# A two-bank PSUM tile for the exponentials of two places in a selective-scan kernel

## The chip, the cores and the metric

The kernel runs on one core of a Trainium2 chip. The metric is device time in microseconds (us), the median of the runs shown. Five engines are spoken of: PE (TensorE, matmuls; PEld is its weight load), DVE (VectorE), ACT (ScalarE), POOL (GpSimd) and SP (SyncE, which issues the DMAs). SBUF is the on-chip memory; PSUM is the accumulator memory, used here as eight banks of 512 fp32 columns on 128 partitions. All data are fp32.

## What is computed

Two layers on an image batch of shape (4, 128, 128, 128). The change lies in the first, a selective-scan ("Mamba") block over the 16,384 tokens of each image, with 256 inner channels and 16 states for each channel. Cut to what matters:

```
u     = silu(causal_conv4(split(x_mlp @ in_proj)))          # 256 channels
dt, B, C = split(u @ x_proj)                                 # 8, 16, 16
delta = softplus(dt @ dt_proj + bias);  A = -exp(A_log)      # A: 256 x 16
h[t,d,s] = h[t-1,d,s] * exp(delta[t,d] * A[d,s]) + delta[t,d] * B[t,s] * u[t,d]
y[t,d]   = sum_s h[t,d,s] * C[t,s] + u[t,d] * D[d]
out   = (y * silu(z)) @ out_proj;   x1 = silu(groupnorm(out)) + x
```

The second layer (group norm, a 1x1 convolution, softmax weights, and a filter in the frequency domain done with matmuls) follows on x1; the change doesn't touch it.

## The kernel before

**Tiling.** Tokens are cut into 128 chunks of T = 512 (32 for each of 4 images). The recurrence has 256 x 16 = 4096 rows for each chunk, as 32 tiles of 128 rows by 512 tokens; a tile has 32 channels by 4 states. They are ordered as 2 halves j of the channels, 4 rotations r, and 4 places p. A place is a group of four states; `place(r, p)` says which group of 32 channels it meets. (j, r) is a *unit* of four tiles, eight units to a chunk, and each unit is two *pairs*: places 0 and 1, then places 2 and 3. So there are 1024 pairs of places 2 and 3 in all.

**Work on one tile.** `exps` (L384): ACT computes exp(delta * A) into a tile da. The tiles of places 1, 2 and 3 are in PSUM, in the pool `psd`, one buffer and one bank each (tags da1, da2, da3); that of place 0 is in SBUF, two buffers. A new tile of the same tag waits until every reader of the old one is done. `dbu` (L352): POOL multiplies delta * u by B for places 1 to 3 into hb; for place 0 PE transposes the product into the PSUM tile b0 (`dbu_turn`, L374). `scans` (L395): DVE runs the recurrence over 512 tokens with one scan instruction per tile (L411), starting from the state that the chunk before left. Then h * C: for places where `by_vector` holds, the scan has written its states in place over da, and DVE multiplies them by C into hb (L413), and ACT copies the last column, the state for the next chunk, into the tile st (L414). For the other places the states lie in an SBUF tile h, POOL multiplies (L418, both places in one instruction of 1024 columns if both are POOL's), and ACT copies the last column later (L506). `sums` (L421): PE adds the four tiles of a unit into y (L432).

`by_vector` (L346) gives places 2 and 3 to DVE, places 0 and 1 to POOL, with two exceptions for balance: in odd chunks without normalisation place 1 of one unit is DVE's, and in the 48 chunks where the group norm of the image before is woven in (`norming`, L337), place 2 of one unit is POOL's.

**Order.** The schedule is written out by hand. A loop over *slots* n, one for each pair, issues the phases "turn", "sums", "pe", "exps", "late", "act", "pool", "dbu", "early", "gate", "scans", "dve", "end" in this order (L502 to L506), and each engine works through its instructions in the order of issue. The exponentials of a pair are issued one slot before its scans, place 0's three slots before. In a slot of places 2 and 3 DVE gets: scan 2, scan 3, multiply 2, multiply 3. On ACT, the two copies of a pair's last columns are issued in its slot, and the exponentials of places 2 and 3 of the next unit follow in the next slot. Between them stand ACT's other steps of the chunk that is being prepared: silu (L238, L241), softplus (L274), the scaling of transposed products (L303), copies out of PSUM. Each switch between exp, silu and softplus is an ACT_TABLE_LOAD.

**Waits.** The framework puts in the semaphore waits: an instruction waits for the last writer of what it reads, and for readers of what it overwrites, on its own engine too. In the listing of the built program, multiply 2 waits for scan 2, multiply 3 for scan 3, each copy (L414) for the multiply that reads the same PSUM tile, and each exponential of places 2 and 3 for the copy that released its tile.

Of the kernel before, what the change touches and what calls it, by code (L numbers as in the profile page):

```python
# [26 lines left out]
F32 = mybir.dt.float32  # L27
AF = mybir.ActivationFunctionType
ALU = mybir.AluOpType
# [4 lines left out]
P = 128  # L34
T = 512
# [119 lines left out]
def block0(tc, s):  # L155
    nc, B, NCH, NH, NS, NG, ND, R, NX, KC, HALO, C, L, NF, DI = (
        s.nc, s.B, s.NCH, s.NH, s.NS, s.NG, s.ND, s.R, s.NX, s.KC, s.HALO, s.C, s.L, s.NF, s.DI,
    )
    NT = T // P
    with ExitStack() as ctx:  # L160
        def pool(name, bufs, **kw):
            return ctx.enter_context(tc.tile_pool(name=name, bufs=bufs, **kw))

        p1 = pool("p1", 1)
        p2 = pool("p2", 2)
# [6 lines left out]
        psd = pool("psd", 1, space=PSUM)  # L172
# [168 lines left out]
        def place(r, p):  # L341


            return (p - r) % ND

        def by_vector(k, j, r, p):  # L346

            if norming(k):
                return p > 1 and (j, r, p) != (1, 2, 2)
            return p > 1 or (k % 2 == 1 and (j, r, p) == (1, 2, 1))  # L350
# [16 lines left out]
        def pair(n):  # L367

            k, r = divmod(n, NP)
            u, p = divmod(r, ND // 2)  # L370
            j, r = divmod(u, NG)
            return k, j, r, 2 * p
# [11 lines left out]
        def exps(n, qs):  # L384

            k, j, r, p = pair(n)
            d = st[k]
            for q in qs:
                m = place(r, p + q)
                c = (j * NG + p + q) * ND + m  # L390
                da = (psd if p + q else p2).tile([P, T], F32, tag=f"da{p + q}", name=f"da{p + q}_{k}_{j}_{r}")
                nc.scalar.activation(da, d["delta", j][:, m, :], AF.Exp, scale=s.amat[:, c : c + 1])  # L392
                d["da", j, r, p + q] = da

        def scans(n):  # L395


            k, j, r, p = pair(n)
            d = st[k]
            hb = d["hb", j, r]  # L400
            das = [d.pop(("da", j, r, p + q)) for q in range(2)]
            dve = [q for q in range(2) if by_vector(k, j, r, p + q)]
            pool = [q for q in range(2) if q not in dve]
            last = d["last", j, r, p] = tiny.tile([P, 2], F32, tag=f"st{j}_{r}_{p}", name=f"st_{k}_{j}_{r}_{p}")
            if pool:
                h = p2.tile([P, 2, T], F32, tag="h", name=f"h_{k}_{j}_{r}_{p}", bufs=3)
            for q in range(2):
                b = hb[:, p + q, :] if p + q else d.pop("b0")
                init = 0.0 if k % NCH == 0 else st[k - 1]["last", j, r, p][:, q : q + 1]
                o = das[q] if q in dve else h[:, q, :]  # L410
                nc.vector.tensor_tensor_scan(o, das[q], b, init, ALU.mult, ALU.add)  # L411
            for q in dve:
                nc.vector.tensor_tensor(hb[:, p + q, :], das[q], d["C"][:, p + q, :], ALU.mult)  # L413
                nc.scalar.copy(last[:, q : q + 1], das[q][:, T - 1 : T])  # L414
            if pool:
                q = slice(pool[0], pool[-1] + 1)
                ps = slice(p + pool[0], p + pool[-1] + 1)
                nc.gpsimd.tensor_tensor(hb[:, ps, :], h[:, q, :], d["C"][:, ps, :], ALU.mult)  # L418
                todo[n + 1, "late"].append(partial(nc.scalar.copy, last[:, q], h[:, q, T - 1]))
# [71 lines left out]
        for n in range(n_chunks * NP):  # L491
            if n % 2 == 0:
                todo[n - 3, "early"].append(partial(exps, n, (0,)))
            todo[n - 1, "exps"].append(partial(exps, n, (1,) if n % 2 == 0 else (0, 1)))
            todo[n - 1, "turn"].append(partial(dbu_turn, n))
            todo[n, "scans"].append(partial(scans, n))
            if n % 2 == 0:
                todo[n - 2, "dbu"].append(partial(dbu, n // 2))
            else:
                todo[n + 2, "sums"].append(partial(sums, n // 2))  # L500
# [483 lines left out]
```

## Time and profile before

| | |
|---|---|
| Median of 3 runs | 7226.67 us (7223.53 to 7229.71) |
| Profiled execution, span from first to last instruction | 7219.4 us (its time apart from the span isn't given) |
| DVE busy | 6925.4 us, 96% |
| POOL busy | 6890.8 us, 95% |
| ACT busy | 6133.6 us, 85% |
| PE busy | 5935.8 us, 82% |
| Exponentials, L392 (ACT) | 4096 of 698 ns |
| Scans, L411 (DVE) | 4096 of about 1260 ns |
| Multiplies by C on DVE, L413 | 2040 of 672 ns |
| Copies of last columns, L414 (ACT) | 2040 of 159 ns |

A group row of the profile has the source line, engine and operation, the tiles written and read with their shapes, the count, then the busy time (us) and the mean duration of one (ns), then the engine's idle time just before them and what ended it. A timeline row has the start in us, the time from the first start to the last end, the line and operation, and the count of equal instructions that were merged into the row; in brackets stands the wait before it. Neighbouring instructions of one engine overlap a little: the profile's end of one lies after the start of the next where the next doesn't need its result.

### The profile page before, as it was taken

What the parts mean: (1) busy time and instruction counts of PE and PEld (TensorE: products, weight loads), DVE (VectorE), ACT (ScalarE), POOL (GpSimd) and SP (SyncE); (2) the same over time, 40 slices, a digit from 0 to 9 for tenths busy, and PEclk for the clock granted to TensorE, in tenths of its full rate; (3) what the DMA queues carried; (4) which work ended last, traced back from release to release, by engine and by line L of the source; (5) the groups of instructions that cost most, each with busy time, mean ns of one, the idle gap of its engine ahead of it and who ended that gap; (6) DMA issues with size and microseconds to landing.
All of it is one profiled execution on the core that took longest, in us unless ns stands there. A gap on an engine that the chain in (4) does not pass through costs nothing. (4 is left out here: it accounts for less than half of the span.)

```text
span 7219.4 us, 89408 instructions
## 1 busy us (share of the span) xinstructions
PE 5935.8 (82%) x25908; PEld 2629.2 (36%) x25908; DVE 6925.4 (96%) x8040; ACT 6133.6 (85%) x13583; POOL 6890.8 (95%) x3188
## 2 busy tenths in 40 slices
PE   7888888888878788888788788887787888868999
PEld 2333333322222233332222233332232323348999
DVE  7999999999999999999999999999999999978677
ACT  7888888888888888888888888888888888877876
POOL 7999999999999999999999999999999999977787
PEclk8888888888888898998888899998888898989999
DMA  6766676677777776777777777777787777768666
GB/s 151 160 159 160 151 165 159 151 165 172 180 192 178 182 172 161 175 169 170 190 179 192 174 160 176 171 160 187 179 192 181 169 173 169 161 167 240 183 169 164
DMA packets 864127, 1246.27 MB, mean 173 GB/s; under 512 B 78856, under 2 KB 318608, under 8 KB 863632
## 3 DMA queue, kind: packets, MB, share of 16 engines
q1 hardware_dynamic: 863488, 1240.28, 71.8%
q8 instruction: 204, 3.34, 0.2%
q14 instruction: 291, 2.38, 0.1%
q10 hardware_dynamic: 144, 0.26, 0.0%
HBM read 996.97 MB, written 243.27 MB: 172 GB/s over the span
## 5 line engine op out<-in xcount | busy, mean ns | idle before, releaser
L362 POOL TENSOR_TENSOR hb<-rdu,rB 128x1536 f32<-128x1536 f32 (+2 forms) x1536 | 3608.0, 2366 | 35.1 <-DMA rdu<-dd 32.1
L392 ACT ACTIVATE da<-rdelta,amat 128x512 f32<-128x512 f32 x4096 | 2786.1, 698 | 139.3 <-DVE h L411 134.5
L418 POOL TENSOR_TENSOR hb<-h,rC 128x1024 f32<-128x1024 f32 (+1 forms) x1072 | 2436.8, 2275 | 68.4 <-DVE h L411 53.9
L411 DVE TENSOR_TENSOR_SCAN da<-da,st,hb 128x512 f32<-128x512 f32 x1976 | 2417.4, 1265 | 22.1 <-ACT da L392 15.6
L432 PE MATMUL y<-hb,sel 128*32 128x512 f32 x8192 | 1337.9, 730 | 4.7 <-POOL hb L418 4.1
L382 PE MATMUL b<-ident,bt 128*128 128x128 f32 x4096 | 753.9, 307 | 673.5 <-DVE h L411 539.1
L413 DVE TENSOR_TENSOR hb<-da,rC 128x512 f32<-128x512 f32 x2040 | 1294.3, 672 | 3.0
L411 DVE TENSOR_TENSOR_SCAN h<-da,st,b 128x512 f32<-128x512 f32 x992 | 1256.2, 1266 | 1.5 <-PE b L382 1.5
L411 DVE TENSOR_TENSOR_SCAN h<-da,st,hb 128x512 f32<-128x512 f32 x1000 | 1249.9, 1254 | 1.4 <-ACT da L392 1.0
L233 PE MATMUL pp_cv<-xm,wck 128*128 128x512 f32 x2048 | 1061.0, 665 | 1.4 <-ACT xm L216 0.8
L303 ACT ACTIVATE bt<-pt_dut,xdt 128x256 f32<-128x256 f32 x2048 | 836.3, 470 | 186.0 <-PE pt_dut L292 185.8
L382 PEld LDWEIGHTS b<-ident,bt 128*128 128x128 f32 x4096 | 525.5, 154 | 1242.1 <-DVE h L411 902.5
L414 ACT COPY st<-da 128x1 f32<-128x1 f32 x2040 | 271.3, 159 | 495.0 <-DVE hb L413 494.7
L233 PEld LDWEIGHTS pp_cv<-xm,wck 128*128 128x128 f32 x2048 | 417.3, 215 | 706.5 <-issue 460.8
L767 POOL TENSOR_TENSOR wb<-wb,term 128x1040 f32<-128x1040 f32 x192 | 461.1, 2402 | 89.8 <-ACT term L761 78.6
L292 PE MATMUL pt_dut<-ident,du 128*128 128x128 f32 x1024 | 233.7, 339 | 299.9 <-ACT xdt L285 174.0
L428 PE MATMUL y<-u,diag 128*128 128x512 f32 x512 | 300.9, 671 | 149.7 <-DVE zs L442 147.6
L292 PEld LDWEIGHTS pt_dut<-ident,du 128*128 128x128 f32 x1024 | 132.5, 163 | 618.6 <-POOL du L311 492.3
L392 ACT ACT_TABLE_LOAD x262 | 336.1, 1283 | 11.8 <-DMA rdelta<-dd 7.1
L311 POOL TENSOR_TENSOR du<-delta,u 128x512 f32<-128x512 f32 x256 | 319.6, 1271 | 26.7 <-ACT delta L274 26.7
L432 PEld LDWEIGHTS y<-hb,sel 128*32 128x32 f32 x8192 | 173.3, 116 | 371.4 <-issue 278.0
L266 PE MATMUL pp_dt<-xd,wdt 8*128 8x512 f32 x512 | 281.9, 639 | 31.9 <-ACT pp_o L456 23.4
(145 smaller groups left out, 8082.0 us busy)
## 6 DMA issues: line engine op xcount, KB each, us to landing
rdelta<-dd SPq DMA_DIRECT2D x1024, 256.0 KB, 4.7
rdu<-dd SPq DMA_DIRECT2D x1024, 256.0 KB, 7.8
rC<-bc SPq DMA_DIRECT2D x512, 256.0 KB, 7.5
rB<-bc SPq DMA_DIRECT2D x512, 192.0 KB, 4.7
dd<-delta SPq DMA_DIRECT2D x256, 256.0 KB, 7.4
dd<-du SPq DMA_DIRECT2D x256, 256.0 KB, 5.9
ft<-in_filt_w SPq DMA_DIRECT2D x104, 520.0 KB, 6.9
ob<-o SPq DMA_DIRECT2D x128, 256.0 KB, 2.0
```

The costliest lines, as they stand in the source:

```text
L233: nc.tensor.matmul(ps["cv", j], w, d["xm"][:, t : t + T], start=t == 0, stop=t == KC - 1)
L292: nc.tensor.transpose(ps["dut"][:, 2 * t + j, :], d["du"][:, j, at : at + P], s.ident)
L303: nc.scalar.activation(d["bt"][:, 2 * h + t, :, q, :], src, AF.Copy, scale=d["xdt"][:, 2 * h + t, R + q : R + q + 1])
L311: nc.gpsimd.tensor_tensor(du, d["delta"][:, j, :], d["u"][:, j, :], ALU.mult)
L362: nc.gpsimd.tensor_tensor(hb[:, p : p + n, :], d["du", j][:, m : m + n, :], d["B"][:, p - 1 : p - 1 + n, :], ALU.mult)
L382: nc.tensor.transpose(b[:, t * P : (t + 1) * P], src, s.ident)
L392: nc.scalar.activation(da, d["delta", j][:, m, :], AF.Exp, scale=s.amat[:, c : c + 1])
L411: nc.vector.tensor_tensor_scan(o, das[q], b, init, ALU.mult, ALU.add)
L413: nc.vector.tensor_tensor(hb[:, p + q, :], das[q], d["C"][:, p + q, :], ALU.mult)
L418: nc.gpsimd.tensor_tensor(hb[:, ps, :], h[:, q, :], d["C"][:, ps, :], ALU.mult)
L432: nc.tensor.matmul(y[m * DG : (m + 1) * DG, :], s.sel, d["hb", j, r][:, p, :], start=False, stop=r == NG - 1)
L767: nc.gpsimd.tensor_tensor(wb, wb, u[n].terms[f], ALU.add)
```

## The change

The exponentials of places 2 and 3 get one PSUM tile of 128 x 2 x 512 (tag da23, two banks, one buffer) in place of two tiles of one bank each; the number of banks in use stays eight. Place q of the pair is the half `[:, q, :]`. Where both places are DVE's, one multiply of 1024 columns follows the two scans, and one ACT copy takes both last columns. Where only one place is DVE's, the code for it is as it was, on its half of the tile. Places 0 and 1 keep their tiles and their code.

```diff
             for q in qs:
                 m = place(r, p + q)
                 c = (j * NG + p + q) * ND + m
-                da = (psd if p + q else p2).tile([P, T], F32, tag=f"da{p + q}", name=f"da{p + q}_{k}_{j}_{r}")
+                if p == 0:
+                    da = (psd if q else p2).tile([P, T], F32, tag=f"da{q}", name=f"da{q}_{k}_{j}_{r}")
+                else:
+                    if q == 0:
+                        d["pair"] = psd.tile([P, 2, T], F32, tag="da23", name=f"da23_{k}_{j}_{r}")
+                    da = d["pair"][:, q, :]
                 nc.scalar.activation(da, d["delta", j][:, m, :], AF.Exp, scale=s.amat[:, c : c + 1])
                 d["da", j, r, p + q] = da
...
                 o = das[q] if q in dve else h[:, q, :]
                 nc.vector.tensor_tensor_scan(o, das[q], b, init, ALU.mult, ALU.add)
-            for q in dve:
-                nc.vector.tensor_tensor(hb[:, p + q, :], das[q], d["C"][:, p + q, :], ALU.mult)
-                nc.scalar.copy(last[:, q : q + 1], das[q][:, T - 1 : T])
+            if len(dve) == 2:
+                both = d.pop("pair")
+                nc.vector.tensor_tensor(hb[:, p : p + 2, :], both, d["C"][:, p : p + 2, :], ALU.mult)
+                nc.scalar.copy(last, both[:, :, T - 1])
+            else:
+                for q in dve:
+                    nc.vector.tensor_tensor(hb[:, p + q, :], das[q], d["C"][:, p + q, :], ALU.mult)
+                    nc.scalar.copy(last[:, q : q + 1], das[q][:, T - 1 : T])
             if pool:
```

## Prediction

> **What bounds the kernel now.** I read the windows view first, to see which engine is full in which stage; then VectorE's waits inside that stage; then the timeline of VectorE and of ScalarE at single pairs; last, groups by shape for the rate per column. The chain of waits covers only the last 12% of the span (the second layer) and says nothing of the scan stage, so it isn't used.
>
> The scan stage runs from 49 to 6400 us. Its row gives the length, then busy time (and count) of PE, PE's weight loads, DVE, ACT and POOL:
>
> ```profile
> 49.00:6400.00 6351.00, 5158.17 (x19617) 1898.99 (x19616) 6314.61 (x6610) 5492.87 (x12263) 6266.72 (x2862) 0.88 0.73 170
> ```
>
> DVE is idle for 6351.0 - 6314.6 = 36.4 us in 6351, POOL for 84.3. ACT has 858 us free. DVE's own waits in that window name few others (total us, times, longest):
>
> ```profile
> DVE da L411 <- ACT da L392: 17.5, 17, 2.0
> ...
> DVE h L411 <- POOL hb L362: 4.0, 2, 3.7
> DVE da L411 <- POOL hb L362: 2.0, 2, 1.1
> ```
>
> So DVE sets the end of this stage, with POOL close behind. What lengthens DVE's chain comes through whole; what shortens it can bring 84 - 36 = 48 us before POOL is as full as DVE is now. One unit of DVE work, two pairs of places:
>
> ```profile
> 3011.82 1.27 DVE L411 TENSOR_TENSOR_SCAN h<-da,st,b 128x512 f32<-128x512 f32 x1
> 3013.00 1.26 DVE L411 TENSOR_TENSOR_SCAN h<-da,st,hb 128x512 f32<-128x512 f32 x1
> 3014.18 2.44 DVE L411 TENSOR_TENSOR_SCAN da<-da,st,hb 128x512 f32<-128x512 f32 x2
> 3016.53 1.27 DVE L413 TENSOR_TENSOR hb<-da,rC 128x512 f32<-128x512 f32 x2
> 3017.71 1.27 DVE L411 TENSOR_TENSOR_SCAN h<-da,st,b 128x512 f32<-128x512 f32 x1
> ```
>
> Read starts, not durations. Two scans take 16.53 - 14.18 = 2.35 us, 1.175 each, though one lasts 1.265: the next instruction starts some 0.09 before the last one's end, as it doesn't need its result. Two multiplies take 17.71 - 16.53 = 1.18. The same view at a place where the multiply needs the scan just ahead of it (place 1 on VectorE, in odd chunks):
>
> ```profile
> 3000.47 1.25 DVE L411 TENSOR_TENSOR_SCAN da<-da,st,hb 128x512 f32<-128x512 f32 x1
> 3001.76 0.69 DVE L413 TENSOR_TENSOR hb<-da,rC 128x512 f32<-128x512 f32 x1
> 3002.37 2.46 DVE L411 TENSOR_TENSOR_SCAN da<-da,st,hb 128x512 f32<-128x512 f32 x2
> ```
>
> Here the start to start is 1.29, not 1.175: the overlap is gone. In all 88 such places of the trace the gap after the scan is +33 to +35 ns, against a median of -87 elsewhere. **A hand-off to the very next DVE instruction costs 122 ns.** The kernel before avoids it at places 2 and 3 by the order scan, scan, multiply, multiply.
>
> **What the Trainium skill says.** "VectorE: DVE Perf Modes", the section on the TRN2 errata, has a fixed cost per instruction beside one cycle per column, and gives (N+151)/0.96 ns for an fp32 tensor_tensor: 691 ns at 512. The trace has 672 (2040 of L413); the part of it that is paid per instruction is what one multiply less saves. The same page, "The DRAIN you can't avoid", says that a semaphore after each op costs nothing extra. The trace disagrees, by the 122 ns above, and I take the trace. "PSUM — Partial Sum Buffer", section on bank collisions, wants any two engines kept apart on one bank, reads included. The trace agrees: the state copies, which only read, wait for the multiply that only reads (494.7 us of L414's idle time).
>
> **The change part by part.** In the listing of the built programs, with what each instruction waits for, 976 of the 1024 pairs have both places on VectorE and change in full; in the other 48 (batch chunks with normalisation) place 2 stays on POOL.
>
> 1. *One multiply of 1024 columns for two.* Rate from the two shapes of L820:
>
> ```profile
> L820 DVE TENSOR_TENSOR pr<-sq,wb 128x390 f32<-128x390 f32 x256 | 132.5, 559 | 8.8
> L820 DVE TENSOR_TENSOR pr<-sq,wb 128x260 f32<-128x260 f32 x128 | 48.8, 423 | 2.2
> ```
>
> (559 - 423)/130 = 1.046 ns per column, so 512 more columns add 536 ns to a multiply's pitch of 590: 1126 against 1184 for two. Gain 58 ns; the bounds are 0 (crossing a bank costs as much as an instruction) and 90 (all that a multiply has over its columns is saved, with overlap). I take 58.
>
> 2. *The second scan now waits for the first.* This isn't in the diff. The pair is one tile, and in the listing scan 3 waits for DVE's own count of scan 2, in all 976 pairs (before: none); the two touch different halves. Cost 122 ns, by the row above; bounds 0 (if a scan's result needs no wait, as the skill's sentence has it) and 150. I take 122.
>
> 3. *The multiply now follows the scan that it needs.* Before, one multiply stood between. In the listing all 976 wait for the instruction just ahead. Again 122 ns, same bounds.
>
> Sum on DVE per pair: 122 + 122 - 58 = +186 ns, times 976 = 181.5 us. The 48 other pairs keep their single multiply, already a hand-off, and get only the scan's wait: 48 x 0.122 = 5.9. Together **+187 us**, all on the path. One small wait of DVE for the second old multiply goes; it is done a unit earlier and costs nothing.
>
> 4. *State copy, 976 fewer on ACT.* L414 takes 159 ns, but two together take only 0.20 us, so about 40 to 60 ns each of ACT's time: some 50 us, on an engine with 858 free. Worth nothing by itself.
>
> 5. *Both exponentials wait for the one copy, and scan 2 for both exponentials.* The exponentials of the next unit may start only when the tile is released. Queued behind the waiting exponentials on ACT is everything in its order: silu, softplus, bt scaling, the next place 1. Before, in a quiet unit:
>
> ```profile
> 3011.93 0.16 ACT L414 COPY st<-da 128x1 f32<-128x1 f32 x1 [0.44 <-DVE hb L413]
> 3011.99 1.31 ACT L392 ACTIVATE da<-rdelta,amat 128x512 f32<-128x512 f32 x2
> ```
>
> The multiply ends at 3011.90; after it DVE runs two scans and reaches scan 2 at 3014.18, 2.28 us later. Now: copy 0.03 + 0.16, a hand-off of 0.03 on ACT (DVE's gap; ACT's copy to exponential shows the same), exponential 0.70, hand-off 0.03 (the second waits for the first, also in the listing), 0.70, and 0.03 to DVE: 1.68 us. It fits, with 0.6 to spare, where scan 2 had 1.5 before. The cover is a punctual ACT. It is gone after the table loads:
>
> ```profile
> 3017.88 1.31 ACT L392 ACTIVATE da<-rdelta,amat 128x512 f32<-128x512 f32 x2
> 3019.21 1.28 ACT L241 ACT_TABLE_LOAD   x1
> ...
> 3022.73 1.28 ACT L392 ACT_TABLE_LOAD   x1
> 3024.03 0.69 ACT L392 ACTIVATE da<-rdelta,amat 128x512 f32<-128x512 f32 x1
> ...
> 3025.53 1.30 ACT L392 ACTIVATE da<-rdelta,amat 128x512 f32<-128x512 f32 x2
> ```
>
> ```profile
> 3026.57 1.26 DVE L411 TENSOR_TENSOR_SCAN da<-da,st,hb 128x512 f32<-128x512 f32 x1
> ```
>
> The last two exponentials start at 3025.53, 1.24 after their multiply's end. The first is done at 3026.22, in time for 3026.57; the second, serial, at about 3026.96. Scan 2 then starts near 3026.99, 0.42 late. Both chains shift by nearly the same before that (ACT some 0.2 by its later start, DVE 0.19 by points 1 to 3), so the lateness stays. I made this sum for all 1023 successive pairs of the trace: (start of the exponentials, at least 0.23 after the multiply's end) + 1.46 - (start of scan 2). It is positive in 244: 123 at (half 1, rotation 0), after softplus, 0.28 each; 77 at (0, 2), after silu, 0.43 each; 27 at (1, 2), 0.61 each; 17 elsewhere. Sum **96 us**, bounded by 0 (DVE's slower pace gives ACT time) and 170 (0.3 more for each of the 244).
>
> 6. *What else moves.* POOL, PE and DMA issue the same instructions in the same order per unit and all get slack; DVE's waits for POOL (6 us) go. No queue is passed by a moved DMA.
>
> Sum: 187 + 96 - 6 = +277 us. The profiled execution spans 7219.4, 7.3 below the median of the three runs shown, 7226.67, so the difference is added to the median: **7504 us**.
>
> **Rivals.** *Hand-offs alone* (+187 - 6): ACT catches up because DVE is slower. For it, ACT has 14% free; against, the late units are late by bursts of table loads, not by the average. 7408. *Punctual ACT runs out*: the 0.6 us of slack is also eaten in quiet units by ACT work that sits ahead of the copy, say 0.1 us at the other 780: +277 + 78, 7582. Against it: the median start of the exponentials is 90 ns after the multiply. *Faster*: the hand-offs overlap after all, since the two scans touch different banks, so only the 58 ns of each multiply counts: -57 us, of which 48 fit before POOL is as full as DVE was; 7175. It decides if two hand-offs cost less than 58 ns, 29 each; the 88 places at +35 ns speak against it. That the two products are not merged is excluded by the listing (976 multiplies of 1024).
>
> **Chances.** Forecast 0.66, with its own range 7440 to 7560; hand-offs alone 0.16; ACT running out 0.12; faster 0.04; within 0.2% of no change (hand-offs at a quarter of their price) 0.02. A measurement here can tell about 0.2%, 14 us, from no change. The range reaches to 7400, takes in the hand-offs alone, and to 7580: it leaves out faster, same and most of the third case. Slower 0.94, same 0.02, faster 0.04.
>
> **What would show it.** In the changed trace: the multiply of 1024 columns at 1.21 us, starting some 35 ns after scan 3's end; scan 3 as far behind scan 2; scan 2 to the next scan 0 at 3.72 us, not 3.53; DVE's waits for ACT near 100 us, up from 19, mostly at two of the eight units of a chunk; POOL's busy share in the stage down to about 94%. If the scans still start 1.175 apart, points 2 and 3 are wrong and the sum with them; if DVE's waits for ACT stay at 20 us, point 5 is.

## The result, and the profile after

The changed kernel takes 7580.37 us (median, 7578.58 to 7584.86) against 7225.45 for the kernel before in the same session: a ratio of 1.0492, 95% interval 1.0479 to 1.0505, or 355 us more. The forecast was 277 us more, 7504; the measured time lies 0.4 us above the end of the range, 7580, and 76 us above the forecast itself. The direction and the mechanisms came as forecast, and one price, that of a hand-off on DVE, was too low.

The windows view of the scan stage, which now runs from 48 to 6760 us (length, then busy time of PE, weight loads, DVE, ACT and POOL):

```profile
48.00:6760.00 6712.00, 5315.78 (x19616) 1940.45 (x19618) 6507.55 (x5635) 5559.38 (x11288) 6275.63 (x2862) 0.85 0.68 161
```

The stage is 361 us longer. POOL's busy time is what it was within 9 us, so it isn't the bound: its share fell to 93.5%. DVE is busy for 193 us more, with 975 instructions fewer, and idle for 6712.0 - 6507.6 = 204 us where it was idle for 36. Its waits in the stage, by what ended them (only gaps over 0.15 us are listed):

```profile
DVE da L416 <- ACT da L397: 40.4, 40, 2.3
...
DVE da L416 <- issue: 33.9, 79, 1.2
DVE da L416 <- POOL hb L362: 20.5, 18, 1.6
```

All three are scans of places 2 and 3. What is put down to "issue" belongs mostly to ACT's bursts too: without table loads, below, that row falls from 33.9 to 8.4. The rest of DVE's 204 us is in gaps too short for this view. The timeline of one quiet unit of DVE (no burst on ACT, nothing else between the scans) shows them; the row after it, two scans of the unit that follows, is used further below:

```profile
3008.77 1.27 DVE L416 TENSOR_TENSOR_SCAN h<-da,st,b 128x512 f32<-128x512 f32 x1
3009.95 1.26 DVE L416 TENSOR_TENSOR_SCAN h<-da,st,hb 128x512 f32<-128x512 f32 x1
3011.13 2.59 DVE L416 TENSOR_TENSOR_SCAN da<-da,st,hb 128x512 f32<-128x512 f32 x2
3013.76 1.22 DVE L419 TENSOR_TENSOR hb<-da,rC 128x1024 f32<-128x1024 f32 x1
3014.90 1.27 DVE L416 TENSOR_TENSOR_SCAN h<-da,st,b 128x512 f32<-128x512 f32 x1
...
3017.26 2.66 DVE L416 TENSOR_TENSOR_SCAN da<-da,st,hb 128x512 f32<-128x512 f32 x2
```

The first two scans start 1.18 apart, as before. Scan 2 to the multiply, two hand-offs, takes 13.76 - 11.13 = 2.63 us where it took 2.35. The multiply of 1024 columns takes 14.90 - 13.76 = 1.14 where two took 1.18. The unit takes 6.13 us where it took 5.89. On ACT the chain from the released tile to the next unit's scan 2 is there as costed:

```profile
3015.01 0.16 ACT L420 COPY st<-da 128x2 f32<-128x2 f32 x1 [1.05 <-DVE hb L419]
3015.21 1.42 ACT L397 ACTIVATE da<-rdelta,amat 128x512 f32<-128x512 f32 x2
```

The multiply ends at 3014.98; the copy starts 0.03 later, the two exponentials lie end to end (1.42, not 1.31) and end at 3016.63, in time for scan 2 at 3017.26 in this unit.

**Where the time went.** Summing starts to starts over the 1023 units that have a successor, in both traces, splits the stage without a rest (where there are two multiplies, "its multiply" is the first):

| from start to start | before, us | after, us | difference | forecast |
|---|---|---|---|---|
| scan 0 to scan 1 | 1218.2 | 1216.6 | -1.6 | 0 |
| scan 1 to scan 2 (ACT late) | 1414.2 | 1520.3 | +106.1 | +96 |
| scan 2 to scan 3 | 1206.3 | 1358.4 | +152.1 | +125 |
| scan 3 to its multiply | 1205.8 | 1354.2 | +148.4 | +119 |
| multiply to the next scan 0 | 1301.3 | 1257.2 | -44.1 | -57 (and -6, POOL) |
| sum | 6345.9 | 6706.7 | +360.8 | +277 |

### The profile page after: what moved, and what is told of

It reads as the page before. It is cut to its first block, busy times and chain, and to the rows that moved or that the text cites. A ratio compares the mean times of both kernels' runs of the same rounds, so it can differ in the third digit from the quotient of the medians.

```text
span 7576.8 us, 86828 instructions
## 1 busy us (share of the span) xinstructions
PE 6091.0 (80%) x25908; PEld 2668.1 (35%) x25908; DVE 7117.8 (94%) x7064; ACT 6200.2 (82%) x12607; POOL 6899.9 (91%) x3188
## 5 line engine op out<-in xcount | busy, mean ns | idle before, releaser
L397 ACT ACTIVATE da<-rdelta,amat 128x512 f32<-128x512 f32 x4096 | 2867.7, 700 | 173.2 <-DVE h L416 102.7
L416 DVE TENSOR_TENSOR_SCAN da<-da,st,hb 128x512 f32<-128x512 f32 x1976 | 2537.6, 1284 | 153.8 <-ACT da L397 35.2
L382 PE MATMUL b<-ident,bt 128*128 128x128 f32 x4096 | 782.7, 315 | 880.7 <-DVE h L416 730.6
L442 PE MATMUL y<-hb,sel 128*32 128x512 f32 x8192 | 1395.6, 759 | 3.6 <-DVE hb L419 2.7
L419 DVE TENSOR_TENSOR hb<-da,rC 128x1024 f32<-128x1024 f32 x976 | 1195.0, 1224 | 33.2
L233 PE MATMUL pp_cv<-xm,wck 128*128 128x512 f32 x2048 | 1091.5, 681 | 1.4 <-ACT xm L216 0.8
L420 ACT COPY st<-da 128x2 f32<-128x2 f32 x976 | 152.2, 156 | 706.9 <-DVE hb L419 706.7
L397 ACT ACT_TABLE_LOAD x262 | 336.1, 1283 | 12.0 <-DMA rdelta<-dd 7.4
```

The lines of the kernel that those rows point to most:

```text
L233: nc.tensor.matmul(ps["cv", j], w, d["xm"][:, t : t + T], start=t == 0, stop=t == KC - 1)
L382: nc.tensor.transpose(b[:, t * P : (t + 1) * P], src, s.ident)
L419: nc.vector.tensor_tensor(hb[:, p : p + 2, :], both, d["C"][:, p : p + 2, :], ALU.mult)
L442: nc.tensor.matmul(y[m * DG : (m + 1) * DG, :], s.sel, d["hb", j, r][:, p, :], start=False, stop=r == NG - 1)
```

## The experiments

A hand-off is, as in the prediction, the wait of an instruction for the one just ahead of it on DVE; such an instruction is called held. Theory A: the loss is two hand-offs on DVE for each pair, at about 150 ns each and not 122, and ACT's lateness behind bursts. Theory B: the hand-off is its gap alone, 122 ns. Theory C: hand-offs are cheap and ACT's lateness is the loss.

**Two multiplies again.** The changed kernel with the shared tile and the one copy, and the product undone:

```diff
-                nc.vector.tensor_tensor(hb[:, p : p + 2, :], both, d["C"][:, p : p + 2, :], ALU.mult)
+                for q in dve:
+                    nc.vector.tensor_tensor(hb[:, p + q, :], das[q], d["C"][:, p + q, :], ALU.mult)
```

> The changed kernel with its shared two-bank tile and its single copy, but with two multiplies of 512 columns again. It keeps the scan's hand-off, one hand-off into a multiply and the shared release of the tile, and undoes only the merged product. If the merging brings what the rate per column says (58 ns for each of 976 pairs), this kernel takes 57 us more than the changed one, 7637 us; if a multiply over two banks brings nothing, it takes the same 7580. In both theories the second multiply, which needs nothing from the first, overlaps with it.

Measured 7632.83 us, 52 more than the changed kernel. In its trace the way from scan 3 to the next scan 0 grew by 62.8 us, 64 ns for a pair, and the wait ahead of scan 2 shrank by 8. So the merged product does bring its small gain; it is outweighed.

**Hand-offs alone.** The kernel before, with the order of DVE's work changed in a full pair from scan, scan, multiply, multiply to scan, multiply, scan, multiply:

```diff
                 nc.vector.tensor_tensor_scan(o, das[q], b, init, ALU.mult, ALU.add)
-            for q in dve:
-                nc.vector.tensor_tensor(hb[:, p + q, :], das[q], d["C"][:, p + q, :], ALU.mult)
-                nc.scalar.copy(last[:, q : q + 1], das[q][:, T - 1 : T])
+                if q in dve:
+                    nc.vector.tensor_tensor(hb[:, p + q, :], das[q], d["C"][:, p + q, :], ALU.mult)
+                    nc.scalar.copy(last[:, q : q + 1], das[q][:, T - 1 : T])
```

> The kernel before with its separate tiles, in the order scan 2, multiply 2, scan 3, multiply 3 on DVE: two hand-offs into a multiply for each of 976 pairs and nothing else of the change (one hand-off is there already in the other 48). Theory A (a hand-off costs its gap of 122 ns and a longer life of the held instruction, 16 ns for a multiply): 276 ns for a pair, 269 us in all, 7495 us. Theory B (the gap alone, as in the forecast): 244 ns, 238 us, 7463 us. Theory C (DVE's hand-offs are cheap and the changed kernel's loss is ACT's late exponentials): under 100 us, below 7325. The release of the tiles for ACT comes earlier than before, so no wait for ACT is expected in A or B.

Measured 7499.06 us against 7224.27, 275 more (ratio 1.0381, 1.0366 to 1.0397). This fits theory A, and not B or C. No data, tile or instruction changed, only who stands ahead of whom. The way from scan 2 to the next scan 0 grew by 289.7 us for 2 x 976 hand-offs, 148 ns each; the wait ahead of scan 2 shrank by 7.5. DVE's timeline of one pair and the next scan 0:

```profile
3001.00 1.27 DVE L411 TENSOR_TENSOR_SCAN da<-da,st,hb 128x512 f32<-128x512 f32 x1
3002.30 0.69 DVE L413 TENSOR_TENSOR hb<-da,rC 128x512 f32<-128x512 f32 x1
3002.91 1.28 DVE L411 TENSOR_TENSOR_SCAN da<-da,st,hb 128x512 f32<-128x512 f32 x1
3004.23 0.69 DVE L413 TENSOR_TENSOR hb<-da,rC 128x512 f32<-128x512 f32 x1
3004.84 1.27 DVE L411 TENSOR_TENSOR_SCAN h<-da,st,b 128x512 f32<-128x512 f32 x1
```

Scan to multiply is 1.30 and 1.32 here, not 1.175; and the held multiply to the next scan is 0.61, not 0.59, as the multiply itself lasts 0.69 and not 0.67. The second of these is what the forecast left out. A small part here is something else: scan 3, which isn't held, stands behind a multiply and lasts 1283 ns at the median, where scan 2 behind a scan lasts 1268. That is 15 ns of a pair's 297.

**ACT's bursts.** Relu in place of silu and softplus, which leaves these functions out, in both kernels:

```diff
-                    nc.scalar.activation(u[:, j, :], ps["cv", j], AF.Silu, bias=s.cb[:, j : j + 1])
+                    nc.scalar.activation(u[:, j, :], ps["cv", j], AF.Relu, bias=s.cb[:, j : j + 1])
...
-                nc.scalar.activation(d["zs"], d["zs"], AF.Silu)
+                nc.scalar.activation(d["zs"], d["zs"], AF.Relu)
...
-                    nc.scalar.activation(delta[:, j, :], ps["dt", j], AF.Softplus, bias=s.bdt[:, j : j + 1])
+                    nc.scalar.activation(delta[:, j, :], ps["dt", j], AF.Relu, bias=s.bdt[:, j : j + 1])
```

> The changed kernel with Relu in place of silu and softplus in the chunks' preparation (L238, L241, L274), which leaves those functions out and with them four ACT table loads in most chunks; the work on DVE stays. If the lateness of scan 2 behind the second exponential (96 us in the forecast, the same in the trace after) comes from these bursts, this kernel gains most of it: about 7580 - 90 = 7490 us. If the exponentials are late because the tile is released late in every unit, it stays near 7580.

> The kernel before with the same Relu in place of silu and softplus, as the pair of the run without table loads of the changed kernel. DVE waited 19 us for ACT here, so about 7210 us. The difference of the two kernels without table loads is then DVE's own share of the change: theory A (gap and longer life) 258 ns for 976 pairs and about 150 for 48, 259 us; theory B (gaps alone) 187 us.

Measured 7497.59 us for the changed kernel (83 less than with its tables) and 7225.02 for the kernel before (no less: its waits for ACT, 19 us, weren't of this kind, a miss of 15 us). The pair differs by 272.6 us, not by 355. From scan 1 to scan 2 the pair differs by 1437.2 - 1417.6 = 19.6 us, where the full kernels differ by 106.1. So 86 of the 106 us of lateness come from table loads and what stands between them. Without the 19.6 us, 253 us of the pair's difference are left for DVE's own hand-offs and multiply: theory A had 259, B had 187.

DVE's waits in the stage without table loads, to set beside those shown above:

```profile
DVE da L416 <- ACT da L397: 30.3, 23, 2.3
DVE da L416 <- POOL hb L362: 8.9, 8, 1.6
DVE da L416 <- issue: 8.4, 11, 0.9
```

**The release window.** The multiply put after the next unit's scan 0, so that it isn't held, and the exponentials of places 2 and 3 issued after it:

```diff
+                if p == 0 and q == 0 and held:
+                    held.pop()()
...
+                def product():
+                    nc.vector.tensor_tensor(hb[:, p : p + 2, :], both, d["C"][:, p : p + 2, :], ALU.mult)
+                    nc.scalar.copy(last, both[:, :, T - 1])
+                held.append(product)
-                nc.vector.tensor_tensor(hb[:, p : p + 2, :], both, d["C"][:, p : p + 2, :], ALU.mult)
-                nc.scalar.copy(last, both[:, :, T - 1])
...
-            todo[n - 1, "exps"].append(partial(exps, n, (1,) if n % 2 == 0 else (0, 1)))
+            todo[n - 1, "exps" if n % 2 == 0 else "dve"].append(partial(exps, n, (1,) if n % 2 == 0 else (0, 1)))
```

> The changed kernel with its tile in PSUM, with the multiply put after the next unit's scan 0 and the exponentials of places 2 and 3 issued after it in ACT's order. The multiply's hand-off goes (150 ns for each of 976 pairs), but the time from the multiply's end to scan 2 shrinks to one scan, 1.1 us, where copy, two exponentials and their hand-offs take 1.68. If that chain is as the forecast has it, scan 2 is 0.58 us late in nearly every unit: 7580 - 146 + 590 = about 8020 us, less up to 96 us since the bursts of ACT now run ahead of it. If the chain overlaps more than that, under 7600.

Measured 8439.77 us: the direction, but 420 us more than expected. In quiet units the chain is what it was taken for. DVE, then ACT:

```profile
3698.97 1.20 DVE L424 TENSOR_TENSOR hb<-da,rC 128x1024 f32<-128x1024 f32 x1
3700.09 1.27 DVE L417 TENSOR_TENSOR_SCAN h<-da,st,hb 128x512 f32<-128x512 f32 x1
3701.85 2.69 DVE L417 TENSOR_TENSOR_SCAN da<-da,st,hb 128x512 f32<-128x512 f32 x2 [0.49 <-ACT da L398]
```

```profile
3700.21 0.16 ACT L425 COPY st<-da 128x2 f32<-128x2 f32 x1 [1.51 <-DVE hb L424]
3700.40 2.02 ACT L398 ACTIVATE da<-rdelta,amat 128x512 f32<-128x512 f32 x3
```

From the multiply's end, 3700.17, to scan 2 at 3701.85 pass 1.68 us, the very sum of the forecast. Scan 2 follows scan 1 by 1.76, not 1.175: 0.58 late. The excess is in three units of a chunk, (0, 1), (0, 3) and (1, 2), written (half, rotation), where the median from scan 1 to scan 2 is 4.14, 3.04 and 3.66 us, and 1.75, 1.18 and 1.18 in the changed kernel. There other work of ACT lengthens the chain: at (0, 1) and (0, 3) a table load stands between the copy and the exponentials, and at (1, 2), often at (0, 1) too, other steps stand ahead of the copy. That I expected the bursts to run ahead of it was wrong. What it shows is that the 1.68 us are a real chain, and that place in ACT's order matters, not its load alone.

**In SBUF.** If the tile lies in SBUF, the framework keeps its halves apart (in the listing scan 3 no longer waits for scan 2), and two buffers fit. Room for them was made by one buffer less for h and o; that alone is the base.

```diff
-                        d["pair"] = psd.tile([P, 2, T], F32, tag="da23", name=f"da23_{k}_{j}_{r}")
+                        d["pair"] = p2.tile([P, 2, T], F32, tag="da23", name=f"da23_{k}_{j}_{r}")
```

> The kernel before with one buffer less for the tiles h and o (two in place of three), which makes the room in SBUF that the next kernels need. It is their base. If POOL is never more than one unit behind DVE, about 7225 us; if DVE has to wait for h, up to 0.1 us for each of 1024 units, 7330 us.

> As the base, with the exponentials of places 2 and 3 in SBUF, two buffers each, as two separate tiles and with two multiplies: no hand-off of the change, only the place of the data. Without contention for SBUF, as the base, 7225 us or up to 20 us less since ACT is never held up by a release. If VectorE's two SBUF inputs shut POOL out, as the Trainium skill's page SBUF - State Buffer says of instructions with two SBUF inputs, the 3.5 us of scans and multiplies of a unit no longer lie beside POOL's 5.7 us: far over 8000 us.

> As the base, with the changed kernel's shared tile, one multiply and one copy, but the tile in SBUF with two buffers. There the scans' halves are kept apart: scan 3 waits for nothing of scan 2, only the multiply's hand-off remains, and the exponentials have a unit more of time. Theory A, without contention: 150 for the hand-off less 44 for the merged product, 976 times: 104 us over its base, about 7330 us, and no wait for ACT. If the changed kernel's loss is bound to the merged multiply alone, near 7580. With contention it follows the run with separate tiles in SBUF.

> As the shared tile in SBUF, with the multiply put after the next unit's scan 0, so that no instruction of these needs the one just ahead. Theory A without contention: 44 ns gained for each of 976 pairs, 43 us under its base, about 7182 us, and POOL nearly full. Theory of a merged product that brings nothing: as the base. With contention it follows the run with separate tiles in SBUF.

The base took 7268.71 us (DVE waited 45 us for h). Separate tiles in SBUF: 12236.86. The shared tile in SBUF: 11644.85, and with the delayed multiply 11291.67. The groups of scans and of POOL's products in the kernel before:

```profile
L411 DVE TENSOR_TENSOR_SCAN da<-da,st,hb 128x512 f32<-128x512 f32 x1976 | 2417.4, 1265 | 22.1 <-ACT da L392 15.6
L362 POOL TENSOR_TENSOR hb<-rdu,rB 128x1536 f32<-128x1536 f32 (+2 forms) x1536 | 3608.0, 2366 | 35.1 <-DMA rdu<-dd 32.1
```

And the groups of the run with separate tiles:

```profile
L411 DVE TENSOR_TENSOR_SCAN da<-da,st,hb 128x512 f32<-128x512 f32 x1976 | 5038.7, 2587 | 0.0
L362 POOL TENSOR_TENSOR hb<-rdu,rB 128x1536 f32<-128x1536 f32 (+2 forms) x1536 | 4753.0, 3107 | 21.2 <-DMA rdelta<-dd 21.2
L413 DVE TENSOR_TENSOR hb<-da,rC 128x512 f32<-128x512 f32 x2040 | 3614.5, 1808 | 3.1
L411 DVE TENSOR_TENSOR_SCAN h<-da,st,b 128x512 f32<-128x512 f32 x992 | 1257.5, 1268 | 0.0
```

Scans of places 2 and 3, now with two SBUF inputs, last 2587 ns on the mean where they lasted 1265; the scan of place 0, with b0 in PSUM, lasts 1268 as before. The multiplies went from 672 to 1808, POOL's products from 2366 to 3107. That is the contention that the Trainium skill describes ("SBUF — State Buffer", Who interferes with whom): a VectorE instruction with two SBUF inputs contends with a GpSimd one that reads SBUF. The trace agrees, and it isn't that SBUF is slow by itself: the 637 multiplies beside which POOL ran nothing lasted 658 to 689 ns. The three runs say little of hand-offs: both the shared tile and the delay are faster than the separate tiles, but fewer and longer instructions under contention may be the reason, and that wasn't separated.

**A version that uses the finding.** The kernel before, with the scan of the place that DVE multiplies put first where a pair has only one such place:

```diff
-            for q in range(2):
+            for q in dve + pool if len(dve) == 1 else range(2):
```

> The kernel before, with one line changed: where a pair has only one place on DVE (88 pairs: 48 with place 3, 40 with place 1), that place's scan goes first and the other's second, so that the multiply no longer follows the scan it needs. The trace of before has exactly these 88 hand-offs. Theory A (a hand-off costs about 150 ns): 13 us less than before, 7212 us. Theory B (122 ns): 11 us less. If a hand-off costs nothing on the path, no difference.

Measured 7210.42 us against 7223.66 (ratio 0.998, 0.9972 to 0.9988): 13 us less, the only version here that beats both kernels. The interval, 9 to 20 us, shows that a hand-off costs time on the path, but it doesn't tell 13 from theory B's 11. It takes out the very 88 hand-offs from which the forecast had its price. DVE's timeline at such a pair, with place 1:

```profile
2996.72 1.28 DVE L411 TENSOR_TENSOR_SCAN da<-da,st,hb 128x512 f32<-128x512 f32 x1
2997.91 1.25 DVE L411 TENSOR_TENSOR_SCAN h<-da,st,b 128x512 f32<-128x512 f32 x1
2999.09 0.66 DVE L413 TENSOR_TENSOR hb<-da,rC 128x512 f32<-128x512 f32 x1
2999.67 2.46 DVE L411 TENSOR_TENSOR_SCAN da<-da,st,hb 128x512 f32<-128x512 f32 x2
```

Its multiply starts 1.18 after the scan ahead of it, not 1.29, and lasts 0.66, not 0.69. From the first scan of such a pair to the instruction after its multiply, three starts on, the median fell by 143 to 144 ns, so the trace sides with A.

## Why the prediction was right, and where it was wrong

*The bound*: right. DVE's chain came through whole; POOL got slack.

*Point 1, the merged multiply*: right in kind, a little large. The undone product cost 64 ns for a pair in its own run; from before to after the typical way from the first multiply to the next scan 0 went from 1185 to 1141 ns, 44 gained and not 58. The merged multiply is held, and lasts 16 ns longer than the rate per column gave; so most of these 14 ns are the hand-off's, and the rate itself was right (held multiplies of 512 and 1024 columns differ by 532 ns, the forecast had 536).

```profile
L419 DVE TENSOR_TENSOR hb<-da,rC 128x1024 f32<-128x1024 f32 x976 | 1195.0, 1224 | 33.2
```

The skill's formula that I quoted and set aside, (N+151)/0.96, gives 691 and 1224 ns: these are the durations of held multiplies to the nanosecond or two (690 to 693 in the alternating order, 1224 in the changed kernel). The 672 of the trace before is the duration of one that overlaps its neighbour.

*Points 2 and 3, the two hand-offs*: right that they are there, and **wrong in price, the step that failed**. "I take 122" was the gap alone. A held instruction also lasts longer: scan 3 went from a median of 1262 ns to 1291, the multiply gained its 16. It stood in the rows that the prediction showed: the multiply after its scan has 0.69 and the next scan starts 0.61 later, against 0.67 and 0.59. With that, each hand-off is 148 ns (alternating order), inside the bound of 150 that I kept for the range, not the value taken. The changed kernel agrees: in quiet units the median from scan 2 to scan 3 went from 1175 to 1303 ns and from scan 3 to the multiply from 1175 to 1325; with the multiply's 16 that is 294 for the two.

There is a second term that I hadn't seen: in all 256 pairs of rotation 3 the gap from scan 2 to scan 3 is 103 ns or more, in the other 720 it is 34 to 36. It is why the two scans of the row at 3017.26 take 2.66 us and those at 3011.13, in rotation 2, 2.59. In the listing, scan 3 waits there for POOL as well as for scan 2, since in that rotation POOL makes the product of place 3 as a piece of its own. 68 ns, 256 times, is 17 us. In the trace, an instruction of DVE's sequencer (EVENT_SEMAPHORE) stands ahead of scan 3 in just these 256 pairs, and it carries the wait for scan 2. The trace before has the same two gaps in the second layer: 103 or 104 ns for the 64 products of L820 with such an instruction ahead of them, 34 or 35 for the 128 without. It isn't the number of waits: 128 merged multiplies have a sequencer instruction ahead that waits for transfers, carry the wait for their scan themselves, and start after 34 or 35 ns. This is read from the traces; no run removed the second wait.

Together the two rows of hand-offs cost 300.5 us and not 244. What scan 3's wait for scan 2 costs wasn't tried alone in PSUM either; its gap, 34 to 36 where it was -89, is that of the multiply's hand-off.

*Point 4, the copies*: worth nothing, as said; ACT's load was never the bound. Its busy time in the stage even rose, by 67 us: the two exponentials no longer overlap (1.42 us for two, not 1.31), and 0.11 us in each of 976 pairs outweighs what the copies save.

*Point 5, ACT late*: right in place and nearly in size, 106 us against 96, and 86 of it goes with the table loads. In the changed trace scan 1 to scan 2 at (0, 2), after silu, is 1488 ns on the mean where it was 1199, at (1, 0), after softplus, 1480 where it was 1230.

*Point 6*: the 6 us of waits for POOL didn't go but grew, by what the waits view puts down to POOL, to 24 us. The hand-offs alone were a rival at 7408, and its two halves fell differently: the hand-offs cost more, and ACT didn't catch up. *Punctual ACT runs out* gave 7582, near the measured time, but by luck, for a reason that the traces contradict: at the quiet rotation (0, 3) the median from scan 1 to scan 2 is 1175 ns, as it was.

So the sum missed by 84 us in the profile: 27 + 29 in the hand-offs, 13 in the multiply (its own longer life as a held instruction), 10 in ACT, and some 5 in the rest. Some 69 of the 84 are thus the price of a hand-off, 17 of them the wait that stands apart.

## What to carry to other kernels

Before merging two instructions of a full engine, look at who stands ahead of the merged one: the merge saves one fixed cost (here 44 to 64 ns) and may make the result of the instruction just ahead a need, and a hand-off costs more (148 ns here). Where independent work is at hand, put it between producer and consumer, as the old order did and as the 13 us of the reordered mixed pairs show. And price a hand-off from starts three instructions long, not from the gap: the held instruction lasts longer too. A tile shared by two producers is also released, filled and waited for as one.

## What the runs showed of the hardware that was not expected

An instruction of VectorE held behind the one just ahead reads longer in the profile by 19 to 29 ns (multiply 672 to 691, scan 1262 to 1291), so durations of one and the same instruction differ with its neighbours. The Trainium skill's "VectorE: DVE Perf Modes", The DRAIN you can't avoid, found the semaphore free in a row of eight copies, and says too that an instruction that isn't held starts earlier. This case has the price of that difference: 1952 waits for the instruction just ahead cost 275 us in a stream that would overlap. A wait for the instruction just ahead cost 34 to 36 ns after its end where the waiting instruction carried it, and 103 to 105 where a sequencer instruction did (nearly all of the 256 scans above, and 64 products in the second layer). Two SBUF inputs beside a full POOL doubled a scan (1265 to 2587 ns) and slowed POOL too (2366 to 3107): the place of the exponentials in PSUM is worth far more in this kernel than any saving in instructions tried here.
